# Feed-forward part of a two-layer sequence kernel: pairs of chunks on 64x64 tiles of the PE array

## The chip, the cores and the metric

The kernel runs on one core of one Trainium2 chip. The metric is the device time of one execution in microseconds (us); the time of a kernel is the median of its runs. PE is the matrix engine (TensorE), PEld its weight loads, DVE the vector engine, ACT the scalar engine, POOL GpSimd, SP the queue from which most loads are issued. All data are fp32.

## The reference

The input x is 4 batches x 512 time steps x 128 frequencies x 64 channels (a row of 8192 features for each time step). Layer 0 is a sequence block, layer 1 a spectral one. Cut to what matters:

```
# layer 0, for each batch
xn = layernorm(x);  k, v, r = xn@Wk, xn@Wv, sigmoid(xn@Wr)       # 8192 -> 64 each
states = scan(s = decay*s + k*v);  x = x + (r*states)@Wo          # projection, scan, attention
x = x + gelu(conv_freq(layernorm(x)))                             # 3 taps over frequency
x = x + layernorm(conv_time(layernorm(x)))                        # 3 causal taps over time, per feature
mid = gelu(x @ ffn_W1 + ffn_b1)                                   # 64 -> 256 for each (time, frequency)
x = x + (mid @ ffn_W2 + ffn_b2)                                   # 256 -> 64
# layer 1: moving average (25 steps) + 128 Fourier modes mixed over frequency, then back
```

The change is in the last two lines of layer 0.

## The kernel before

`layer0` keeps data with features on partitions. A chunk is 128 features (2 frequencies x 64 channels) x 512 time steps; there are 64 chunks a batch, and most steps take pairs of chunks (32 pairs). Layer 0 is cut into stages, each a Python generator that issues instructions and yields a weight: J `project` (8192 to k, v, r), Z `scan`, A `attend_and_convolve`, C `convolve_time`, O `open_feed` (residual of the first two pairs), F `feed_forward`. `in_turn` runs two of them side by side, always the one that is behind, with a small lead for the second stream. The order of matmuls is therefore written by hand; the instructions of the other engines are put in order by the scheduler, except those pinned with `keep_in_program_order`. The pairing of stages is:

| first stream | second stream |
|---|---|
| Z(0), A(0) | J(1), Z(1) |
| C(0) | A(1) |
| O(0), F(0) | J(2), Z(2) |
| C(1) | A(2) |
| O(1), F(1) | J(3), Z(3) |
| C(2) | A(3) |
| O(2), F(2) | C(3), O(3) |
| F(3) | nothing |

Then `layer1` runs, from DRAM.

**F before.** For each chunk c, `widen(c, m)` for m = 0, 1 multiplies each half of the chunk (one frequency, 64 channels, so 64 rows of the array) by 128 of the 256 middle features: two matmuls of 64 rows x 128 columns into the two banks of a double PSUM tile, m from pool `ps_m` (tile m) or `ps_c` (tile c), L718. ACT makes the GELU of 128x1024 into `mid` (L722, 4 buffers). `narrow(c-1)` multiplies back: four matmuls of 128 rows x 64 columns, summed over m, into the one bank of `ps_p` (tile pa, L729); DVE adds bias and residual into `x4t` (L734, `scalar_tensor_tensor`). `store(c-2)` transposes x4t in four 128x128 matmuls (tile pt, L743) into the bank s of `ps_s` if the attention stage does not hold it (`free_s`), else into that of `ps_p`; ACT copies them to `ob` (L752, or in halves L750), and POOL issues one DMA for each four chunks (L754). Between them `residual` (L686, L687 on DVE) and `add_residual` (L695 on ACT, L698 on DVE) make the input x3 two pairs ahead.

In F(0) and F(1) each second chunk also advances `convolve_ahead(b + 1)`: 14 pairs of the next time convolution, made early by DVE (L608, L611, L620) and ACT (L616), with the rows for it spread by PE into the bank of `ps_p` (L241). In C, `add_up` sums values and squares by matmuls with a block of ones (L251). In A, `convolve` uses tiles m and c too (L547 for the norm's correction, L556 for neighbouring halves with 64x64 weights, L561 for the chunk itself), and the sums go into bank s. The eight PSUM banks are: `ps_a` 2, `ps_c` 2, `ps_m` 2, `ps_s` 1, `ps_p` 1.

Of the kernel before, what the change touches and what calls it, by code (L numbers as in the profile page):

```python
# [16 lines left out]
P = 128  # L17
# [62 lines left out]
def layer0(ctx, tc, dram, x, xt, vecs, wkvr, wo, wdec, wconv, fbias, w1, fb1, w2, fb2, x4):  # L80
# [73 lines left out]
    tb_all = const.tile([P, NCH], F32, name="tb_all")  # L154
    fix = const.tile([P, NCH, 2], F32, name="fix")
# [12 lines left out]
    def prepare():  # L168
# [45 lines left out]
        t01 = rowp.tile([P, SL], F32, tag="rg", name="t01")[:, 0:P].rearrange("p (k c) -> p k c", k=2)  # L214
        t0, t1 = t01[:, 0, :], t01[:, 1, :]
        nc.vector.tensor_tensor(t0, vec[:, W0, :], vec[:, B3, :], ALU.mult)
        nc.vector.tensor_tensor(t1, vec[:, W1, :], vec[:, B3, :], ALU.mult)
        nc.vector.tensor_tensor(t1, t1, t0, ALU.add)
        nc.vector.tensor_scalar_mul(fix[:, :, 0], t1, -1.0)
        nc.vector.tensor_scalar_mul(fix[:, :, 1], t0, -1.0)  # L220
        nc.vector.tensor_tensor(tb_all, vec[:, W2, :], vec[:, B3, :], ALU.mult)
        nc.vector.tensor_tensor(tb_all, tb_all, t1, ALU.add)
        nc.vector.tensor_tensor(tb_all, tb_all, vec[:, TB, :], ALU.add)
        for k in (W0, W1, W2):
            nc.vector.tensor_tensor(vec[:, k, :], vec[:, k, :], vec[:, G3, :], ALU.mult)
# [91 lines left out]
    free_s = [True]  # L317
    held = [False]
# [193 lines left out]
    def attend_and_convolve(b):  # L512
# [62 lines left out]
        for i in range(NPR + 3):  # L575
# [8 lines left out]
            if 1 < i < NPR + 2:  # L584
                convolve(i - 2)
                yield 5.0
            if i == 3:
                st = ps_s.tile([P, SL], F32, tag="s", name="st")
                free_s[0] = False
# [39 lines left out]
    def convolve_ahead(b):  # L629


        rb, mb = yield from rows(of_p, *carried[b], "rm3")
        ahead[b] = rb, mb
        for i in range(AHEAD):
            xr = spare("x1", SL)
            normed(b, i, xr, xr, rb, mb, True)
            yield
            tapped(b, i, xr, spare("z", SL), True)
            yield
# [69 lines left out]
    def feed_forward(b):  # L709
        x3s = opened.pop(b)  # L710
        mids, x4s, obs = {}, {}, {}

        def widen(c, m):
            x3 = x3s[c // 2][:, c % 2, :]
            pm = c_bank() if m else two(ps_m, "m")
            for h in range(2):
                hs = slice(h * H, (h + 1) * H)
                nc.tensor.matmul(  # L718
                    pm[:, h, :], lhsT=w1_sb[hs, m * P : (m + 1) * P], rhs=x3[hs, :], start=True, stop=True
                )  # L720
            mid = mids[c, m] = bk.tile([P, 2, SL], F32, tag="mid", name="mid", bufs=4)
            nc.scalar.activation(mid, pm, AF.Gelu_apprx_tanh, bias=fb1_sb[:, m : m + 1])  # L722

        def narrow(c):
            pa = ps_p.tile([P, SL], F32, tag="p", name="pa")
            for m in range(2):
                mid = mids.pop((c, m))
                for h in range(2):
                    nc.tensor.matmul(  # L729
                        pa[h * H : (h + 1) * H, :], lhsT=w2_sb[:, m, :], rhs=mid[:, h, :],  # L730
                        start=(m == 0), stop=(m == 1),
                    )
            x4t = x4s[c] = bk.tile([P, SL], F32, tag="x4t", name="x4t", bufs=3)
            nc.vector.scalar_tensor_tensor(x4t, pa, fb2_sb, x3s[c // 2][:, c % 2, :], ALU.add, ALU.add)  # L734
            if c % 2:
                x3s.pop(c // 2)

        def store(c):
            x4t = x4s.pop(c)
            pool, tag = (ps_s, "s") if free_s[0] else (ps_p, "p")  # L740
            pt = pool.tile([P, NT, P], F32, tag=tag, name="pt")
            for t in range(NT):
                nc.tensor.transpose(pt[:, t, :], x4t[:, t * P : (t + 1) * P], ident)  # L743
            s = c // 4
            if c % 4 == 0:
                obs[s] = bk.tile([P, NT, SL], F32, tag="ob", name="ob")
            o = obs[s][:, :, c % 4 * P : (c % 4 + 1) * P]
            if c // 2 % 2:
                for h in range(2):
                    nc.scalar.copy(o[:, :, halves[1 - h]], pt[:, :, halves[h]])  # L750
            else:
                nc.scalar.copy(o, pt)  # L752
            if c % 4 == 3:
                nc.gpsimd.dma_start(  # L754
                    x4[b][:, s * SL : (s + 1) * SL].rearrange("(t p) d -> p t d", p=P), obs.pop(s)
                )

        early = None
        for c in range(NCH + 2):
            if c < NCH:  # L760
                widen(c, 0)
                widen(c, 1)
            i = c // 2 + 2
            if i < NPR:
                if c % 2:
                    x3s[i] = add_residual(b, i, *coming)
                else:
                    coming = residual(b, i)
            if 0 < c <= NCH:
                narrow(c - 1)  # L770
            if c > 1:
                store(c - 2)
            if b + 2 < B and c > 4 and c % 2:
                early = early or convolve_ahead(b + 1)
                next(early, None)
            yield 4.5
# [40 lines left out]
    def nothing(b):  # L817
# [7 lines left out]
        F: 4.5 * (NCH + 2), nothing: 1.0,  # L825
# [253 lines left out]
def _inputs(x, i):  # L1079
# [22 lines left out]
    for rows, parts in ((MODES, ("w_real", "w_imag")), (IMAG, ("w_imag", "w_real"))):  # L1102
# [14 lines left out]
        "fb1": i["ffn_b1"].reshape(2, P).T,  # L1117
        "w2": i["ffn_W2"].reshape(2, P, H).transpose(1, 0, 2),
# [22 lines left out]
```

## Time and profile before

| what | value |
|---|---|
| median of 3 runs | 3773.87 us (3772.81 to 3791.47) |
| span of the profiled execution | 3800.7 us; the page gives no other time of that execution |
| PE busy | 3636.3 us (96% of the span) |
| DVE, ACT, POOL busy | 2683.6, 1761.2, 513.3 us |
| F(0), F(1): first to last L718 matmul | 839.3 to 1224.2, 1498.0 to 1878.4 us |
| F(2) and F(3) | 2146.6 to 2788.0 us |
| layer 1 | from about 2796 us to the end |

An engine's busy time is the time in which at least one of its instructions runs. Matmuls are pipelined and their ends are modelled, so the record of a 512-wide matmul is longer (0.59 us) than the distance to the next on the same part of the array. An fp32 matmul of 512 columns leaves two records with one weight load each; a transpose leaves one. "64*128" after a matmul's tiles is the part of the array that it uses, rows*columns. Lines of the profile (L718) are lines of the kernel before.

### The profile page before, as it was taken

How to read it: one execution, taken by the hardware profiler on the slowest of the kernel's cores; microseconds unless marked ns; L12 is line 12 of the kernel's file. 1: busy time of each engine (PE TensorE's matmuls, PEld its weight loads, DVE VectorE, ACT ScalarE, POOL GpSimd, SP SyncE). 2: the span in 40 equal slices, each digit the busy share in tenths (PEclk: the TensorE clock that was granted, in tenths of full speed). 3: DMA queues.
4: the chain of work that ended last, by engine and by line, in shares of the span. 5: the costliest groups of instructions: out<-in, count | busy, mean ns of one | idle time of the engine just before them, and what ended most of it. 6: DMA issues, size and time to landing. Idle time of an engine off the chain costs nothing. (4 is left out here: it accounts for less than half of the span.)

```text
span 3800.7 us, 44873 instructions
## 1 busy us (share of the span) xinstructions
PE 3636.3 (96%) x15945; PEld 1345.5 (35%) x15945; DVE 2683.6 (71%) x3498; ACT 1761.2 (46%) x2491; POOL 513.3 (14%) x782
## 2 busy tenths in 40 slices
PE   9989999999999999999999988999989999999998
PEld 4433322223333223333322322333322843327533
DVE  4445559976777896677789799755567277892677
ACT  0013336645656565566656678867744210142100
POOL 0000012210011221011122221100012000131001
PEclk9999989999999899999999999999999999999999
DMA  9867647786874788787478677545567478993687
GB/s 310 272 203 242 229 146 264 254 288 241 287 280 169 247 285 287 251 278 278 172 258 282 205 249 262 202 155 177 183 222 246 146 236 295 309 294 140 205 296 264
DMA packets 429175, 912.80 MB, mean 240 GB/s; under 512 B 33240, under 2 KB 83608, under 8 KB 424856
## 3 DMA queue, kind: packets, MB, share of 16 engines
q1 hardware_dynamic: 351024, 636.87, 49.7%
q0 software_dynamic: 75776, 271.62, 20.5%
q8 instruction: 127, 2.08, 0.2%
q10 hardware_dynamic: 2152, 1.45, 0.1%
q14 instruction: 96, 0.79, 0.1%
HBM read 641.31 MB, written 268.50 MB: 239 GB/s over the span
## 5 line engine op out<-in xcount | busy, mean ns | idle before, releaser
L729 PE MATMUL pa<-mid,w_sb 128*64 128x512 f32 x2048 | 500.2, 609 | 37.2 <-DVE x4t L734 37.2
L734 DVE SCALAR_TENSOR_TENSOR x4t<-pa,fb_sb,x 128x512 f32<-128x512 f32 x252 | 188.4, 748 | 345.7 <-PE pa L729 345.6
L722 ACT ACTIVATE mid<-m,fb_sb 128x1024 f32<-128x1024 f32 x256 | 285.1, 1114 | 280.5 <-PE m L718 280.2
L718 PE MATMUL m<-x,w_sb 64*128 64x512 f32 x1008 | 290.4, 649 | 0.4 <-ACT mid L722 0.4
L722 ACT ACTIVATE mid<-c,fb_sb 128x1024 f32<-128x1024 f32 x256 | 283.2, 1106 | 1.5 <-PE c L718 1.5
L718 PE MATMUL c<-x,w_sb 64*128 64x512 f32 x1008 | 263.4, 596 | 1.3 <-ACT mid L722 1.3
L729 PEld LDWEIGHTS pa<-mid,w_sb 128*64 128x64 f32 x2048 | 125.0, 136 | 379.9 <-issue 250.8
L406 PE MATMUL a<-xp,wx 128*128 128x512 f32 x512 | 240.7, 596 | 0.5 <-DVE me L268 0.5
L986 ACT COPY two<-a 128x512 f32<-128x512 f32 x64 | 37.5, 586 | 425.0 <-PE a L981 425.0
L1009 PE MATMUL b<-xin,avg_sb 128*128 128x512 f32 x512 | 230.8, 593 | 2.3 <-DVE xin L1015 2.3
L1015 DVE TENSOR_TENSOR xin<-b,pm 128x512 f32<-128x512 f32 x256 | 159.1, 684 | 95.6 <-PE b L1012 80.7
L567 ACT ACTIVATE sq<-x 128x1024 f32<-128x1024 f32 x128 | 135.0, 1054 | 180.5 <-DVE x L564 180.5
L620 DVE SCALAR_TENSOR_TENSOR to<-kd,vec,to 128x510 f32<-128x510 f32 (+1 forms) x272 | 197.8, 746 | 16.0 <-ACT to L616 10.4
L695 ACT ACTIVATE kd<-kd,vec 128x512 f32<-128x512 f32 x256 | 193.3, 809 | 3.1 <-DVE kd L687 3.1
L891 DVE COPY xf<-b 128x256 f32<-128x256 f32 x128 | 54.4, 425 | 185.3 <-PE b L955 173.2
L912 DVE TENSOR_TENSOR uv<-xin 128x1024 f32<-128x1024 f32 x128 | 155.4, 1227 | 39.4 <-DMA xin<-x 18.9
L251 PE MATMUL st<-x,ones 128*32 128x512 f32 x512 | 169.4, 611 | 13.3 <-DVE x L564 13.1
L743 PEld LDWEIGHTS pt<-ident,x4t 128*128 128x128 f32 x1024 | 107.7, 141 | 208.7 <-ACT mid L722 152.5
L528 DVE TENSOR_TENSOR x<-a,xp 128x1024 f32<-128x1024 f32 x128 | 156.2, 1220 | 33.6 <-PE a L526 31.1
L620 DVE SCALAR_TENSOR_TENSOR z<-x,vec,z 128x511 f32<-128x511 f32 x240 | 175.8, 745 | 5.7 <-ACT z L616 2.3
L526 PE MATMUL a<-rst,wo_sb 64*128 64x512 f32 x512 | 153.1, 672 | 27.2 <-DVE x L528 23.2
L743 PE MATMUL pt<-ident,x4t 128*128 128x128 f32 x1024 | 168.8, 288 | 1.5 <-ACT ob L750 1.5
(241 smaller groups left out, 6532.8 us busy)
## 6 DMA issues: line engine op xcount, KB each, us to landing
xp<-in_xt SPq DMA_DIRECT2D x256, 512.0 KB
xin<-x SPq DMA_DIRECT2D x128, 1024.0 KB
kh<-to SPq DMA_DIRECT2D x156, 512.0 KB
x<-x POOLq DMA_DIRECT2D x128, 512.0 KB, 4.4
kx<-x SPq DMA_DIRECT2D x128, 512.0 KB
x<-ob POOLq DMA_DIRECT2D x64, 1024.0 KB, 6.3
out<-xin POOLq DMA_DIRECT2D x64, 1024.0 KB, 7.1
x<-x SPq DMA_DIRECT2D x96, 512.0 KB
```

The lines of the kernel that those rows point to most:

```text
L251: nc.tensor.matmul(st[32 * q : 32 * q + 32, :], lhsT=ones, rhs=src[:, j, :], start=first, stop=last,)
L406: nc.tensor.matmul(pa[:, k, :], lhsT=wq[:, j, k * P : (k + 1) * P], rhs=xp[:, j, :], start=first and j == 0, stop=last and j == 1,)
L528: nc.vector.tensor_tensor(x1, at, xp, ALU.add)
L620: tap = nc.vector.scalar_tensor_tensor(to[:, j, k:], xr[:, j, : SL - k], vec[:, w, c], to[:, j, k:], ALU.mult, ALU.add)
L695: tc.keep_in_program_order(nc.scalar.activation(d[:, j, :], d[:, j, :], AF.Identity, bias=vec[:, B4, c], scale=vec[:, G4, c]))
L718: nc.tensor.matmul(pm[:, h, :], lhsT=w1_sb[hs, m * P : (m + 1) * P], rhs=x3[hs, :], start=True, stop=True)
L722: nc.scalar.activation(mid, pm, AF.Gelu_apprx_tanh, bias=fb1_sb[:, m : m + 1])
L729: nc.tensor.matmul(pa[h * H : (h + 1) * H, :], lhsT=w2_sb[:, m, :], rhs=mid[:, h, :], start=(m == 0), stop=(m == 1),)
L734: nc.vector.scalar_tensor_tensor(x4t, pa, fb2_sb, x3s[c // 2][:, c % 2, :], ALU.add, ALU.add)
L743: nc.tensor.transpose(pt[:, t, :], x4t[:, t * P : (t + 1) * P], ident)
L1009: nc.tensor.matmul(po[j], lhsT=avg_sb[:, j, :], rhs=xin[:, j, :], start=True, stop=False)
L1015: nc.vector.tensor_tensor(by_n(xin[:, j, :]), by_n(po[j]), by_c(pm[j % 2][:, j // 2, :]), ALU.add)
```

## The change

F takes pairs of chunks and quarters of the middle features. `widen(i, q)` makes quarter q (64 features) for pair i: four matmuls of 64 rows x 64 columns, one for each row half h (frequency) and column half j (chunk of the pair), into bank h of tile m or c in turn (`unit`); the partitions of the tile are then 64 features of chunk 0 and 64 of chunk 1. `narrow(i, q)` takes the GELU back in four matmuls of 64 x 64: row half j, column half h, into one accumulator for each chunk (banks p and s), over four quarters. They alternate: widen 2, narrow 0, widen 3, narrow 1, widen 0 of the next pair, narrow 2, widen 1 of the next, narrow 3. The eight transposes of a pair come together at the head of an iteration into a tile m or c, one pair behind in F(0) and F(1), two behind in F(2) and F(3) (`lag`); ACT copies both chunks at once. F yields once for each pair. A flag `feeding` keeps the attention stage from bank s while F runs, and F waits until `free_s`. The rows of `convolve_ahead` go to a tile m or c. Weights w2 and bias fb1 are laid out by quarters, and two constant tables, `tb_all` and `fix`, now lie in rows of `vec` that are no longer needed.

```diff
-    tb_all = const.tile([P, NCH], F32, name="tb_all")
-    fix = const.tile([P, NCH, 2], F32, name="fix")
+    tb_all = vec[:, TB, :]
+    fix = vec[:, G3 : B3 + 1, :].rearrange("p k c -> p c k")
...
     free_s = [True]
+    feeding = [False]
...
+            while i == 3 and feeding[0]:
+                yield BLOCKED
             if i == 3:
                 st = ps_s.tile([P, SL], F32, tag="s", name="st")
...
-    def convolve_ahead(b):
-        rb, mb = yield from rows(of_p, *carried[b], "rm3")
+    def convolve_ahead(b, bank):
+        rb, mb = yield from rows(bank, *carried[b], "rm3")
...
     def feed_forward(b):
         x3s = opened.pop(b)
+        mids, x4s, obs, sums2 = {}, {}, {}, {}
+        lag = 1 if b + 2 < B else 2
+        turn = [0]
+        while not free_s[0]:
+            yield BLOCKED
+        feeding[0] = True
+
+        def unit():
+            turn[0] ^= 1
+            return two(ps_m, "m") if turn[0] else c_bank()
...
+        def widen(i, q):
+            x3 = x3s[i]
+            pm = unit()
             for h in range(2):
-                hs = slice(h * H, (h + 1) * H)
-                nc.tensor.matmul(
-                    pm[:, h, :], lhsT=w1_sb[hs, m * P : (m + 1) * P], rhs=x3[hs, :], start=True, stop=True
-                )
-            mid = mids[c, m] = bk.tile([P, 2, SL], F32, tag="mid", name="mid", bufs=4)
-            nc.scalar.activation(mid, pm, AF.Gelu_apprx_tanh, bias=fb1_sb[:, m : m + 1])
+                for j in range(2):
+                    nc.tensor.matmul(
+                        pm[halves[j], h, :], lhsT=w1_sb[halves[h], q * H : (q + 1) * H], rhs=x3[halves[h], j, :],
+                        start=True, stop=True,
+                    )
+            mid = mids[i, q] = bk.tile([P, 2, SL], F32, tag="mid", name="mid", bufs=4)
+            nc.scalar.activation(mid, pm, AF.Gelu_apprx_tanh, bias=fb1_sb[:, q : q + 1])
...
+        def narrow(i, q):
+            if q == 0:
+                sums2[i] = of_p(), ps_s.tile([P, SL], F32, tag="s", name="pb")
+            mid = mids.pop((i, q))
+            for h in range(2):
+                for j in range(2):
+                    nc.tensor.matmul(
+                        sums2[i][j][halves[h], :], lhsT=w2_sb[halves[j], q, :], rhs=mid[halves[j], h, :],
+                        start=q == 0, stop=q == 3,
+                    )
+            if q < 3:
+                return
+            x3 = x3s.pop(i)
+            if lag > 1:
+                pair = spare("wx", 4 * S + SL)[:, :, 0:SL]
+                x4s[i] = [pair[:, j, :] for j in range(2)]
+            else:
+                x4s[i] = [bk.tile([P, SL], F32, tag="x4t", name="x4t", bufs=3) for _ in range(2)]
+            for j, pa in enumerate(sums2.pop(i)):
+                nc.vector.scalar_tensor_tensor(x4s[i][j], pa, fb2_sb, x3[:, j, :], ALU.add, ALU.add)
+
+        def store(i):
+            pt = unit()
+            for j, x4t in enumerate(x4s.pop(i)):
+                for t in range(NT):
+                    nc.tensor.transpose(pt[:, j, t * P : (t + 1) * P], x4t[:, t * P : (t + 1) * P], ident)
...
+            if i % 2:
                 for h in range(2):
-                    nc.scalar.copy(o[:, :, halves[1 - h]], pt[:, :, halves[h]])
-            else:
-                nc.scalar.copy(o, pt)
-            if c % 4 == 3:
+                    nc.scalar.copy(o[:, :, :, halves[1 - h]], pt[:, :, :, halves[h]])
                 nc.gpsimd.dma_start(
                     x4[b][:, s * SL : (s + 1) * SL].rearrange("(t p) d -> p t d", p=P), obs.pop(s)
                 )
+            else:
+                nc.scalar.copy(o, pt)
...
+        widen(0, 0)
+        widen(0, 1)
+        for i in range(NPR + lag):
+            if i >= lag:
+                store(i - lag)
+            if i < NPR:
+                widen(i, 2)
+                narrow(i, 0)
+                widen(i, 3)
+                narrow(i, 1)
+                if i + 2 < NPR:
+                    coming = residual(b, i + 2)
+                if i + 1 < NPR:
+                    widen(i + 1, 0)
+                narrow(i, 2)
+                if i + 1 < NPR:
+                    widen(i + 1, 1)
+                if i + 2 < NPR:
+                    x3s[i + 2] = add_residual(b, i + 2, *coming)
+                narrow(i, 3)
+            if b + 2 < B and i > 1:
+                early = early or convolve_ahead(b + 1, lambda: unit()[:, 0, :])
                 next(early, None)
-            yield 4.5
+            yield 9.0 * (NPR + 1) / (NPR + lag)
+        feeding[0] = False
```

More of the change, by code (lines that the diff above doesn't have):

```diff
@@ L210, in prepare @@
                 nc.scalar.dma_start(cgr[q : q + 2, :, :], cg4[h, j])
-        t01 = rowp.tile([P, SL], F32, tag="rg", name="t01")[:, 0:P].rearrange("p (k c) -> p k c", k=2)
-        t0, t1 = t01[:, 0, :], t01[:, 1, :]
+        t012 = rowp.tile([P, SL], F32, tag="rg", name="t012")[:, 0 : 3 * NCH].rearrange("p (k c) -> p k c", k=3)
+        t0, t1, t2 = t012[:, 0, :], t012[:, 1, :], t012[:, 2, :]
         nc.vector.tensor_tensor(t0, vec[:, W0, :], vec[:, B3, :], ALU.mult)
@@ L218, in prepare @@
         nc.vector.tensor_tensor(t1, t1, t0, ALU.add)
+        nc.vector.tensor_tensor(t2, vec[:, W2, :], vec[:, B3, :], ALU.mult)
+        nc.vector.tensor_tensor(t2, t2, t1, ALU.add)
+        nc.vector.tensor_tensor(tb_all, vec[:, TB, :], t2, ALU.add)
+        for k in (W0, W1, W2):
+            nc.vector.tensor_tensor(vec[:, k, :], vec[:, k, :], vec[:, G3, :], ALU.mult)
         nc.vector.tensor_scalar_mul(fix[:, :, 0], t1, -1.0)
         nc.vector.tensor_scalar_mul(fix[:, :, 1], t0, -1.0)
[L221 to L225, printed above, removed]
     sums = {}
@@ L710, in feed_forward @@
         x3s = opened.pop(b)
[L711 to L715, printed above, removed]
-            for h in range(2):
-                hs = slice(h * H, (h + 1) * H)
-                nc.tensor.matmul(
-                    pm[:, h, :], lhsT=w1_sb[hs, m * P : (m + 1) * P], rhs=x3[hs, :], start=True, stop=True
-                )
-            mid = mids[c, m] = bk.tile([P, 2, SL], F32, tag="mid", name="mid", bufs=4)
-            nc.scalar.activation(mid, pm, AF.Gelu_apprx_tanh, bias=fb1_sb[:, m : m + 1])
@@ L724, in narrow @@
[L724 to L727, printed above, removed]
-                for h in range(2):
[L729 to L749, printed above, removed]
-                    nc.scalar.copy(o[:, :, halves[1 - h]], pt[:, :, halves[h]])
-            else:
-                nc.scalar.copy(o, pt)
-            if c % 4 == 3:
+        mids, x4s, obs, sums2 = {}, {}, {}, {}
@@ new lines, in store @@
+        def store(i):
[3 more added lines that the diff above has]
+                    nc.tensor.transpose(pt[:, j, t * P : (t + 1) * P], x4t[:, t * P : (t + 1) * P], ident)
+            s = i // 2
+            if i % 2 == 0:
+                obs[s] = bk.tile([P, NT, SL], F32, tag="ob", name="ob")
+            o = obs[s][:, :, i % 2 * 2 * P : (i % 2 + 1) * 2 * P].rearrange("p t (j w) -> p j t w", j=2)
+            pt = pt.rearrange("p j (t w) -> p j t w", t=NT)
+            if i % 2:
+                for h in range(2):
+                    nc.scalar.copy(o[:, :, :, halves[1 - h]], pt[:, :, :, halves[h]])
@@ L756, in store @@
                 )
+            else:
+                nc.scalar.copy(o, pt)
         early = None
[L759 to L763, printed above, removed]
-            if i < NPR:
[L765 to L774, printed above, removed]
+        widen(0, 0)
[3 more added lines that the diff above has]
+                store(i - lag)
+            if i < NPR:
+                widen(i, 2)
[14 more added lines that the diff above has]
+                early = early or convolve_ahead(b + 1, lambda: unit()[:, 0, :])
                 next(early, None)
-            yield 4.5
+            yield 9.0 * (NPR + 1) / (NPR + lag)
+        feeding[0] = False
     CHAIN = 6.0
@@ L824, in layer0 @@
         J: 2.0 * NPR, Z: 7 * CHAIN, A: 7.0 * NPR + 3 * CHAIN, C: 7.0 * (NPR + 2) + 3 * CHAIN, O: 4 * CHAIN,
-        F: 4.5 * (NCH + 2), nothing: 1.0,
+        F: 9.0 * (NPR + 1), nothing: 1.0,
     }
@@ L1116, in _inputs @@
         "w1": np.concatenate([i["ffn_W1"]] * 2, axis=0),
-        "fb1": i["ffn_b1"].reshape(2, P).T,
-        "w2": i["ffn_W2"].reshape(2, P, H).transpose(1, 0, 2),
+        "fb1": np.concatenate([i["ffn_b1"].reshape(4, H).T] * 2),
+        "w2": np.concatenate([i["ffn_W2"].reshape(4, H, H).transpose(1, 0, 2)] * 2),
         "fb2": np.concatenate([i["ffn_b2"]] * 2)[:, None],
```

## The prediction

> **What bounds the kernel now.** I read the page's busy times first, then busy time by stage, then PE's instructions in order of time, then who waited for whom. The page says that PE is the engine to look at:
>
> ```profile
> PE 3636.3 (96%) x15945; PEld 1345.5 (35%) x15945; DVE 2683.6 (71%) x3498; ACT 1761.2 (46%) x2491; POOL 513.3 (14%) x782
> ```
>
> A mean over stages with different limits is not enough, so I cut the span at the first and last matmuls of the feed-forward part (columns: stretch, its length, busy time of PE, PEld, DVE, ACT and POOL with instruction counts, clock, DMA share, GB/s):
>
> ```profile
> 839.00:1232.00 393.00, 387.62 (x1569) 146.38 (x1568) 284.59 (x386) 240.90 (x323) 38.77 (x47) 0.99 0.70 249
> ...
> 1498.00:1889.00 391.00, 387.33 (x1561) 145.91 (x1560) 281.61 (x380) 240.48 (x322) 38.99 (x47) 0.99 0.72 250
> ...
> 2146.00:2516.00 370.00, 330.06 (x1580) 114.38 (x1578) 322.31 (x360) 294.50 (x391) 64.06 (x82) 0.97 0.65 225
> 2516.00:2796.00 280.00, 278.19 (x1272) 101.18 (x1272) 150.93 (x150) 212.81 (x283) 11.33 (x16) 1.00 0.46 160
> ```
>
> These are F(0) (beside the projection of batch 2), F(1) (beside that of 3), F(2) (beside the time convolution of 3) and F(3) alone: 1434 us in all. In the first, second and fourth PE is busy 99%. In F(2) it is 89% and DVE 87%; there PE waited 34.7 us for one thing:
>
> ```profile
> PE pa L729 <- DVE x4t L734: 34.7, 29, 3.9
> ```
>
> PE busy is not PE useful. In F(3), one chunk runs from one m to the next (columns: start, length, engine, line, op, tiles, rows*columns of the array used, moving operand, records; a 512-wide fp32 matmul leaves two records):
>
> ```profile
> 2703.55 1.13 PE L718 MATMUL m<-x,w_sb 64*128 64x512 f32 x4
> 2704.51 1.02 PE L718 MATMUL c<-x,w_sb 64*128 64x512 f32 x4
> 2705.47 1.94 PE L729 MATMUL pa<-mid,w_sb 128*64 128x512 f32 x8
> 2707.34 0.65 PE L743 MATMUL pt<-ident,x4t 128*128 128x128 f32 x4
> 2707.92 1.13 PE L718 MATMUL m<-x,w_sb 64*128 64x512 f32 x4
> ```
>
> A chunk takes 4.37 us. One pass over 512 columns is 0.429 us (the chain of waits has L1009, 8 full-array records, at 3.43 us). The 16 widen and narrow records run two at a time, so 8 steps, 3.43 us; from m to pt it took 3.79. The rest is spent where the shape of the array changes: 64*128, 128*64, 128*128, three times a chunk. The trace also has 64*64 tiles (L556) and four abreast in long runs (L251):
>
> ```profile
> 1251.05 1.09 PE L556 MATMUL c<-z,wcs 64*64 64x512 f32 x8
> 1252.07 1.98 PE L561 MATMUL c<-z,wcs 128*128 128x512 f32 x4
> ...
> 1273.32 0.59 PE L251 MATMUL p<-to,ones 128*32 128x512 f32 x1
> ...
> 1273.75 0.59 PE L251 MATMUL p<-kh,ones 128*32 128x512 f32 x1
> ...
> 1274.17 0.59 PE L251 MATMUL p<-kh,ones 128*32 128x512 f32 x1
> ...
> 1274.60 0.59 PE L251 MATMUL st<-x,ones 128*32 128x512 f32 x1
> ```
>
> Eight 64*64 records between two other shapes took 1.02 us: two steps of four (0.86) and **0.16 for one change of shape**. L251 goes from sum to sum and from bank p to bank st at 0.43 a step: within a shape nothing is added.
>
> [...] The new code sends row half h of the widening to bank h and row half j of the narrowing to bank j; L556 is laid out so too and its four run together. [...] ACT is at 76% in F(3) already. [...] The new stream has 64 records in 6.86 us, 107 ns each; the trace has eight 64*64 records with short operands (L190) in 0.41 us, 51 ns each, so I charge nothing.
>
> **The change part by part.**
>
> *Shapes.* Per pair of chunks the array work stays: widening 16 matmuls (32 records, four abreast, 8 steps), narrowing the same, eight transposes. 16 x 0.429 = 6.86 us, as 2 x 3.43 before. Changes of shape fall from six a pair to two: into the transposes and out. (Beside the projection, its full-array matmuls now stand just ahead of the transposes and need no change between; beside the convolution of 3 the sums cost one more, before and after.) Four changes at 0.16 = **0.65 us a pair**. Cross-check for F(3): 6.86 + 0.16 + 0.58 (pt to m) + four more transposes at (0.66 - 0.29)/3 = 0.12 each is 8.08, against 8.74. 128 pairs: **-83 us** gross, 21 a stage.
>
> *Twice as many matmul and weight-load records:* hidden, since L251 loads four weights within each 0.43 us step. If that cover were gone it is the last rival.
>
> *ACT.* Four GELUs a pair stay (1.11 each), r (L695) stays (2 x 0.81). The two (or, with halves swapped, four) copies of a pair's transposes become one 128x1024 (between 0.58, the 128x512 row, and 1.16, two of them; I take 1.00 by L562, 128x1024 from PSUM) or two 128x512 (1.16). That is 7.1 to 7.2 us of a pair's 8.1 in F(3). In the new order the copy stands behind r; the third widening of the pair needs its bank, 2.8 us after the transposes began, and r and copy end at about 2.75. I charge 0.1 x 32 = +3 us.
>
> *F(0), F(1).* ACT also makes the taps of the convolution ahead (14 pairs in each stage). In the new order the first tap stands in front of the GELU of the pair's first widening, and waits for DVE, whose order there is x4t twice (1.5), x3, L608, L686, L611 (1.22 each): ready 6.6 us after the last narrowing. Tap (0.8) and GELU (1.0) end at 8.4; PE wants the bank back at 7.9 (projection 3.43, transposes 1.0, four units of 0.86). 0.6 x 28 = +17 us (0 if DVE runs ahead, 40 if its loads are late).
>
> *Lag of one pair in F(0), F(1):* the transposes follow the narrowing whose x4t they read. The projection (3.43 us) covers DVE's 1.6 us in 28 pairs a stage. In the last five it is gone, and only scan matmuls (about 1 us) stand there: 0.6 x 10 = +6 us, 0 to 20.
>
> *F(2).* DVE needs five 128x1024 operations (1.22) and six 128x512 (0.75) a pair: 10.6 us, PE only 8.1 + 1.0 for the sums. A pair took 370/32 = 11.6. So DVE is next. Two waits on x4t a pair become one, with 2.9 us (sums, transposes, one widening) against 1.6 of x4t. I take 11.1 a pair, 15 us of the 21: +6; bounds 10.6 (gain 31) and 11.6 (none).
>
> *The two accumulators* take bank p and bank s, so the attention stage's sums must wait until a feed-forward ends; in the order of matmuls that come out, no attention step of the next batch lay inside one, before or after: zero. If one did it would wait, not run, and other steps take its place. *Constants:* tb_all and fix move into vec; the same number of 128x64 DVE operations (about 0.2 us), hidden behind the first projection. *Queues:* the same loads on SP (x2 and the causal output, one each a pair) and 64 stores on POOL; the loads of two projection steps come together and have three buffers; zero, and at most a few us.
>
> Sum: -83 + 3 + 17 + 6 + 6 = **-51 us**. The profiled execution spans 3800.7 us, 0.7% over the median of 3773.87; the page names no other time of it. A saving in us moves from one to the other: 3800.7 - 51 = 3750 there, 3723 at the median, -1.4%.
>
> **Rivals.**
>
> *All of it lands* (ACT's taps early, F(2) at DVE's 10.6): -83 - 10 = 3681 at best, about 3690 likely. For: PE busy 99% in three of four stages. Against: ACT at 88% in F(3).
>
> *ACT and DVE eat it.* GELUs late by 1.5 us in the tap pairs (+42), F(2) at 11.6 (+21), F(3)'s copy late by 0.2 (+6): -83 + 69 = 3760, no change. For: PE's wait on x4t in F(2), and DVE's 10.6 of 11.6. Against: in F(0) PE waited for DVE 5.3 us in all. That the change did nothing is the same time: the order of matmuls does change, but work that another engine sets would not show it.
>
> *Slower:* the 0.16 us belongs to every new group of four tiles and not to the shape. Place: each of the eight widen or narrow units of a pair. 8 x (0.86 + 0.16) + 1.06 = 9.2 us against 8.74, +0.46 x 128 = +59, less some 15 that F(2)'s DVE hides: 3818. For: m and c take 0.96 each here, not 0.86, though both are 64*128. Against: L251 at 0.43 across banks and sums; m pays entering, c leaving. It decides from 0.08 us a unit.
>
> **How the numbers follow.** Forecast 0.68, all lands 0.10, eaten 0.14, slower 0.08. Predicted time 3723. Range 3688 to 3768: it takes in "all lands" and "eaten", and leaves out the slower case and the ends of the bounds. 0.5% is 19 us, about what a measurement of this kernel can tell from no change. Faster by more: the first two and a small part of "eaten", 0.79; within: 0.13; slower: 0.08.
>
> **What would show it.** In F(3), a pair at 8.0 to 8.3 us from transposes to transposes, with steps of 0.43 through widenings and narrowings; F(3) 258 to 266 us. F(0) and F(1) at 375 to 387, with PE waits on ACT in the widening where taps run. F(2) at 340 to 365, DVE over 90%. Wrong would be a unit over 0.94 us, or PE busy under 95% in F(0), F(1) or F(3).

## The result, and the profile after

The changed kernel takes 3755.1 us in the median of 4 runs (3751.9 to 3761.8), the kernel before 3773.34 us in the runs beside it: ratio 0.9945, 95% interval 0.9927 to 0.9964. It is faster by about 18 us where 51 were forecast. The profiled execution spans 3752.0 us and took 3753.95. Compared once more (`after_again` below) it gives 0.9928, interval 0.9902 to 0.9954, about 23 us.

PE's busy time fell by 64 us (3636.3 before). The spans of the two profiled executions differ by more than the medians do, 3800.7 against 3752.0 us, in part because the profiled execution of the kernel before reached F(0) late: at 839.3 us, where `e2_coarse` and `e10_cut_before`, the same kernel up to there, took 824.4 and 822.5. So the spans are not compared. The busy times after:

```profile
PE 3572.1 (95%) x20041; PEld 1376.3 (37%) x20041; DVE 2676.7 (71%) x3498; ACT 1762.1 (47%) x2299; POOL 512.5 (14%) x782
```

Cut by stage (columns as before: stretch, length, busy time of PE, PEld, DVE, ACT and POOL, clock, DMA share, GB/s), with F(0), F(1), F(2), F(3) in this order:

```profile
820.00:1217.00 397.00, 377.47 (x2586) 154.91 (x2584) 285.47 (x391) 245.07 (x277) 38.53 (x48) 0.97 0.73 247
1479.00:1867.00 388.00, 371.02 (x2578) 149.94 (x2576) 280.06 (x378) 242.51 (x274) 36.24 (x45) 0.98 0.74 252
2129.00:2490.00 361.00, 324.26 (x2598) 129.68 (x2600) 320.05 (x360) 289.69 (x340) 65.69 (x81) 0.95 0.68 231
2490.00:2753.00 263.00, 262.88 (x2304) 103.03 (x2296) 150.46 (x150) 211.54 (x236) 12.07 (x16) 0.99 0.49 171
```

F(3) fell from 280 to 263 us. F(2) fell by 9. F(0) and F(1), where a third of the saving was expected, stand at 397 and 388 against 393 and 391, and PE is busy 95 and 96% there instead of 99%. Two numbers serve as yardsticks from here on, because they leave out the start of the kernel and layer 1. The first is the stretch from the first widening of F(0) to that of F(2), two feed-forwards and the convolutions after them: 1307.3 us before (1310.2 in `e10_cut_before`, which differs only from F(2) on), 1308.7 after (1302.7 in `after_again`, 1303.4 in `e10_cut_after`). One kernel's stretch thus differs by up to 6 us from execution to execution, and each number is of one execution. The second is F(2) with F(3), to the last transposes: 648.5 before, 623.5 after. **By these the second gained 25 us and the first between nothing and 8**, together somewhat more than the medians' 18 to 23, as one execution may.

F(3) shows the new stream undisturbed. PE's instructions in order of time, one pair from transposes (L762) to transposes; L730 widens, L743 narrows:

```profile
2605.61 1.09 PE L762 MATMUL m<-ident,wx 128*128 128x128 f32 x8
2606.63 1.09 PE L730 MATMUL c<-x,w_sb 64*64 64x512 f32 x8
2607.54 0.60 PE L743 MATMUL p<-mid,w_sb 64*64 64x512 f32 x2
2607.55 0.60 PE L743 MATMUL pb<-mid,w_sb 64*64 64x512 f32 x2
2607.97 0.60 PE L743 MATMUL p<-mid,w_sb 64*64 64x512 f32 x2
2607.98 0.60 PE L743 MATMUL pb<-mid,w_sb 64*64 64x512 f32 x2
2608.42 1.09 PE L730 MATMUL m<-x,w_sb 64*64 64x512 f32 x8
...
2613.73 1.09 PE L762 MATMUL c<-ident,wx 128*128 128x128 f32 x8
```

A pair takes 8.12 and 8.18 us in turn, against 8.74. The narrowing takes 0.88 us from its first record to the next widening, two steps of 0.43 to 0.45: next to nothing is added between groups of four.

F(0) shows where it went. PE's waits from 820 to 1217 us (columns: what PE was about to do, whom it waited for, us in total, times, longest):

```profile
PE a L476 <- DVE wx L472: 4.1, 1, 4.1
PE c L730 <- ACT mid L735: 3.7, 12, 0.6
PE a L241 <- POOL rs L233: 3.5, 1, 3.5
PE m L730 <- ACT mid L735: 2.7, 3, 1.2
PE a L502 <- DVE hs L496: 2.5, 1, 2.5
PE a L503 <- DVE hs L497: 1.4, 1, 1.4
```

Four of the six are steps of the scan Z(2), the stage that follows the projection as second stream. In F(1) the scan Z(3) holds PE up by 7.1, 3.4 and 1.9 us; the longest two, with a line left out between them:

```profile
PE a L494 <- DVE rst L489: 7.1, 1, 7.1
...
PE a L468 <- DVE wx L472: 3.4, 1, 3.4
```

The scan's waits come to about 12 us in each of the two stages. In the kernel before, one scan step waited in each, for 2.9 us in F(0) and 2.4 in F(1). The tail of F(0) in order of time, each wait in brackets at the end of the line that it held up:

```profile
1153.05 2.08 PE L241 MATMUL a<-ident,rs 128*128 128x128 f32 x8 [3.54 <-POOL rs L233]
1155.80 2.08 PE L241 MATMUL a<-ident,mean 128*128 128x128 f32 x8 [0.68 <-ACT rm L285]
1157.67 1.92 PE L762 MATMUL c<-ident,x4t 128*128 128x128 f32 x8
1159.52 1.99 PE L730 MATMUL m<-x,w_sb 64*64 64x512 f32 x8
...
1178.25 1.12 PE L468 MATMUL a<-kvrg,sel 128*128 128x512 f32 x2
1183.43 2.07 PE L476 MATMUL a<-kvrg,sel 64*128 64x512 f32 x2 [4.06 <-DVE wx L472]
1185.43 1.97 PE L762 MATMUL c<-ident,x4t 128*128 128x128 f32 x8
```

Two scan steps stand back to back between two whole pairs of the feed-forward. L476 follows an L468 directly and waits for what DVE makes from it (L472). The first L241 waits for what POOL makes at the scan's start, and the second for ACT's copy of the first. In the kernel before, the second L241 and the first L467 (its L468) came 5.3 us apart (1177.92 and 1183.18) with a chunk between them. The second thing to see is the length of the lines that follow a wait: transposes of 1.92 and 1.97 us and a widening of 1.99, nearly twice the 1.04 and 1.09 that they take in the pairs with projection (the transposes 1.22 right behind the L468 at 1167.66 us). **Here waits of 3.5 and 4.1 us are followed by matmuls at about half speed**, so they cost about twice: after the first two waits, 4.2 us together, the four lines shown take 8.07 us where 4.3 to 4.6 is usual (an L241 without a wait before it takes 1.06 to 1.16), and the granted clock is 0.51 from 1153 to 1162 us and 0.50 from 1183 to 1189. It shows as well after the waits of 2.5 and 1.4 us that L502 and L503 have one after the other: the transposes behind them take 1.97 us, at a clock of 0.50. Two waits of 1.2 us before widenings in the same tail are not followed by it (1.09 us each).

From one set of transposes to the next, the last five pairs of F(0) and F(1) took 57.8 and 57.3 us before, 74.9 and 66.8 after (70.6 and 66.5 in `after_again`), with the same projection and scan matmuls between them: 22 to 27 us lost in ten pairs.

### The profile page after: what moved, and what is told of

Its sections match the earlier page's. It is cut to its first block, busy times and chain, and to the rows that moved or that the text cites. A ratio compares the mean times of both kernels' runs of the same rounds, so it can differ in the third digit from the quotient of the medians.

```text
span 3752.0 us, 52992 instructions
## 1 busy us (share of the span) xinstructions
PE 3572.1 (95%) x20041; PEld 1376.3 (37%) x20041; DVE 2676.7 (71%) x3498; ACT 1762.1 (47%) x2299; POOL 512.5 (14%) x782
## 5 line engine op out<-in xcount | busy, mean ns | idle before, releaser
L743 PE MATMUL p<-mid,w_sb 64*64 64x512 f32 x2048 | 559.1, 596 | 15.5 <-DVE wx L756 14.3
L743 PE MATMUL pb<-mid,w_sb 64*64 64x512 f32 x2048 | 531.6, 596 | 0.7 <-DVE wx L756 0.7
L730 PE MATMUL c<-x,w_sb 64*64 64x512 f32 x2016 | 280.8, 610 | 16.1 <-ACT mid L735 11.9
L730 PE MATMUL m<-x,w_sb 64*64 64x512 f32 x2016 | 280.7, 609 | 6.7 <-ACT mid L735 4.5
L743 PEld LDWEIGHTS p<-mid,w_sb 64*64 64x64 f32 x2048 | 158.7, 135 | 287.8 <-issue 248.9
L623 DVE SCALAR_TENSOR_TENSOR to<-kd,vec,to 128x510 f32<-128x510 f32 (+1 forms) x272 | 197.1, 742 | 12.5 <-ACT to L619 11.2
L251 PE MATMUL st<-x,ones 128*32 128x512 f32 x512 | 168.9, 605 | 11.5 <-DVE x L565 11.5
L701 DVE TENSOR_TENSOR x<-kd,kx 128x1024 f32<-128x1024 f32 x126 | 154.0, 1222 | 32.5 <-ACT kd L698 32.5
L756 DVE SCALAR_TENSOR_TENSOR x4t<-p,fb_sb,x 128x512 f32<-128x512 f32 x64 | 47.9, 748 | 177.2 <-PE pb L743 177.1
```

What stands on the lines that cost most here:

```text
L251: nc.tensor.matmul(st[32 * q : 32 * q + 32, :], lhsT=ones, rhs=src[:, j, :], start=first, stop=last,)
L623: tap = nc.vector.scalar_tensor_tensor(to[:, j, k:], xr[:, j, : SL - k], vec[:, w, c], to[:, j, k:], ALU.mult, ALU.add)
L701: nc.vector.tensor_tensor(x3, d, x2, ALU.add)
L730: nc.tensor.matmul(pm[halves[j], h, :], lhsT=w1_sb[halves[h], q * H : (q + 1) * H], rhs=x3[halves[h], j, :], start=True, stop=True,)
L743: nc.tensor.matmul(sums2[i][j][halves[h], :], lhsT=w2_sb[halves[j], q, :], rhs=mid[halves[j], h, :], start=q == 0, stop=q == 3,)
```

## The experiments

The first theory: **turns**. F now yields once a pair (weight 9.0) instead of once a chunk (4.5). When the projection is used up, five pairs before the end of F(0) and F(1), the scan's chain of small steps alternates with blocks twice as long, and two of its steps fall into one gap. Rivals: the **lag** of one pair for the transposes, which the forecast named; ACT's **taps**; the **shape** changes being worth less than 0.16 us. In kernels that add lines above, line numbers stand one to three higher.

**e1_half.** Half turns once the projection of batch b+2 has ended (`over` is filled at the end of `project`):

```diff
+        weight = 9.0 * (NPR + 1) / (NPR + lag)
         for i in range(NPR + lag):
+            part = 1.0
...
                 narrow(i, 1)
+                if b + 2 in over:
+                    part = 0.5
+                    yield part * weight
...
-            yield 9.0 * (NPR + 1) / (NPR + lag)
+            yield part * weight
```

> Theory (scan tail): once the projection is used up, the coarse turns of a whole pair put the scan's dependent steps beside too little other work; PE waits (19 us in F(0), 17 in F(1)) and then runs at half clock. With turns of half a pair there, F(0) and F(1) get 10 to 18 us shorter each, the sum of PE's waits on DVE and POOL there falls below 8 us each, and the median is 3723 to 3737. Rival (taps in front of GELUs on ACT): those stalls sit in the pairs with projection, so this edit moves nothing, 3750 to 3760. Rival (lag of one pair): nothing moves either, since the transposes still follow their narrowing.

Measured: 3748.18 us, ratio 0.9919, interval 0.9891 to 0.9947, which overlaps that of the changed kernel; the whole missed its 3723 to 3737. F(1) fell from 386.8 to 374.2 us (first widening to last transposes). F(0) did not move: 395.6 against 396.1. Of the scan's long waits there only that on L241 was left (3.5 us), and another took their place, on x4t:

```profile
1195.85 1.09 PE L764 MATMUL c<-ident,x4t 128*128 128x128 f32 x4 [5.93 <-DVE x4t L758]
...
1223.99 1.97 PE L764 MATMUL c<-ident,x4t 128*128 128x128 f32 x8 [3.86 <-DVE x4t L758]
```

The waits on x4t come to 11.3 us in F(0), where the changed kernel had none. So turns explain F(1), and in F(0) another wait stood hidden behind them: that of the transposes for x4t. Whether the lag makes it, or DVE being held up by something else, is for the next runs.

**e2_coarse.** The kernel before, with its own tiles, but turns of two chunks in F(0) and F(1):

```diff
-            yield 4.5
+            if b + 2 >= B:
+                yield 4.5
+            elif c % 2:
+                yield 9.0
```

> The kernel before, on its old tiles, with turns of two chunks in F(0) and F(1) only. Theory (scan tail): the coarse turns alone cost 10 to 18 us in each of the two, so 3793 to 3808 against 3773 before, with PE waits on the scan's DVE and POOL steps at the end of F(0) and F(1). Rivals (taps, lag, or the new tiles themselves cost the gain): no change, 3768 to 3778.

Measured: 3814.94 us, ratio 1.0084, interval 1.0053 to 1.0116. F(0) rose from 392.5 to 403.0, F(1) from 390.5 to 400.3, F(2) with F(3) stayed at 648.1. PE's waits are those of the changed kernel one line up, in F(0):

```profile
PE a L475 <- DVE wx L471: 4.5, 1, 4.5
PE a L241 <- POOL rs L233: 2.0, 1, 2.0
PE a L502 <- DVE hs L496: 1.6, 1, 1.6
```

and in F(1):

```profile
PE a L493 <- DVE rst L488: 5.8, 1, 5.8
PE a L467 <- DVE wx L471: 2.5, 1, 2.5
```

Turns of that length cost about 10 us a stage with nothing else changed, on the old tiles. The median lies above the 3793 to 3808 expected, and the profiled execution (3801.06) is the quickest of the four, so the stages of the others may have lost more.

**e3_split.** Two changes of shape put back in: four transposes, a widening, then the other four.

```diff
         for i in range(NPR + lag):
             if i >= lag:
-                store(i - lag)
+                turned(i - lag, 0)
             if i < NPR:
                 widen(i, 2)
+            if i >= lag:
+                turned(i - lag, 1)
+                store(i - lag)
+            if i < NPR:
                 narrow(i, 0)
```

`turned(i, j)` makes the four transposes of chunk j, `store` the copies.

> The changed kernel with a pair's eight transposes in two groups of four, the second after the pair's first widening: two more changes of shape a pair, 0.16 us each. If a change of shape costs 0.16 us and lies on the path, +0.33 x 32 = +10 us in F(0), F(1) and F(3) each and up to as much in F(2): 3785 to 3797. If the gain of the change was not the shapes, 3750 to 3762.

Measured: 3876.76 us, ratio 1.0258, interval 1.023 to 1.0285: +122 us on the changed kernel, a miss by a factor of three. The price of the shape shows locally in F(3):

```profile
2704.84 0.66 PE L765 MATMUL c<-ident,wx 128*128 128x128 f32 x4
2705.43 1.09 PE L730 MATMUL m<-x,w_sb 64*64 64x512 f32 x8
2706.45 0.66 PE L765 MATMUL c<-ident,wx 128*128 128x128 f32 x4
2707.03 0.64 PE L743 MATMUL p<-mid,w_sb 64*64 64x512 f32 x1
```

From the first transposes to the narrowing it takes 2.19 us; in the changed kernel eight transposes and a widening took 1.93 (2605.61 to 2607.54 above). Two more changes cost 0.26, 0.13 each against the 0.16 of the forecast. Most of the rest is a wait that the edit made. The transposes' tile is held over a widening more, and PE waits for the copies of it, in F(2) and F(3) for:

```profile
PE c L730 <- ACT ob L777: 35.1, 29, 2.4
PE m L730 <- ACT ob L782: 29.7, 29, 2.0
```

These waits come to 65 us in the 64 pairs of F(2) and F(3), where the shapes at 0.26 a pair come to 17, and to 39 us in F(0) and F(1). The local price stands; the total of this kernel says nothing on it.

**e4_taps.** The convolution ahead is issued in the middle of a pair, so that its taps stand behind the GELUs that PE waits for:

```diff
                 if i + 1 < NPR:
                     widen(i + 1, 1)
+                ahead_step(i)
...
-            if b + 2 < B and i > 1:
-                early = early or convolve_ahead(b + 1, lambda: unit()[:, 0, :])
-                next(early, None)
+            if i >= NPR:
+                ahead_step(i)
```

> The changed kernel with the step of the convolution ahead called in the middle of the pair, so that in ACT's order the taps stand behind two GELUs of the pair instead of in front of the first. If the tap stalls (0.25 to 0.6 us in each of 28 pairs) are the loss, F(0) and F(1) get 5 to 8 us shorter each, 3740 to 3746. If the scan tail is the loss, at most 3750 to 3757, and the pair with taps still takes about 11.6 to 12.0 us.

Measured: 3835.12 us, ratio 1.0131, interval 1.0098 to 1.0164; F(0) 428.5, F(1) 423.3. A miss with the wrong sign. DVE now makes its taps ahead of x4t, and with a lag of one pair PE waits for that in pairs that were free of it:

```profile
PE c L762 <- DVE x4t L756: 21.8, 11, 2.0
```

One such wait, and the half speed behind it:

```profile
930.53 1.27 PE L762 MATMUL c<-ident,x4t 128*128 128x128 f32 x8 [1.95 <-DVE x4t L756]
931.73 1.98 PE L730 MATMUL m<-x,w_sb 64*64 64x512 f32 x8
```

This run makes a wait of its own and so can't weigh the taps. The changed kernel can: its pairs with taps take 12.0 to 12.1 us, those without 11.5, which is close to what the forecast charged, so the taps are not what it missed. The lag of one pair holds in F(0) and F(1) only while DVE does x4t first.

**after_again.** The changed kernel as it is, beside the next three.

> The changed kernel as it is, as the yardstick for the runs beside it: 3751 to 3762 us again. F(0) 392 to 398, F(1) 384 to 390, F(2) and F(3) together 620 to 626; the last five pairs of F(0) 70 to 78 us, of F(1) 63 to 70.

Measured: 3758.0 us, ratio 0.9928, interval 0.9902 to 0.9954; F(0) 391.8, F(1) 385.8, F(2) with F(3) 622.7.

**e5_pin.** e1_half, with one DVE wait for a load moved out of the tail of F(0):

```diff
-            scale_weights(0, ws[0])
+            scale_weights(0, ws[0], True)
```

> Half turns as in e1_half, and the scaling of the first weights of the next projection is kept in program order, so that DVE does not meet its load in the tail of F(0). If that load is what made the transposes wait for x4t in e1_half (10.4 us there), F(0) falls by 8 to 13 us against e1_half's 395.6, F(1) stays at 374 and the whole is about 3738. If the lag of one pair is too short in the tail whatever DVE does, F(0) stays within 3 us of 395.6 and the x4t waits stay at about 10 us.

Measured: 3752.8 us, ratio 0.9924, interval 0.9901 to 0.9948. F(0) fell to 386.8 as expected of the load, F(1) is 375.4. The whole did not follow, and missed its 3738: in the stretch from F(0) to F(2) it stands at 1295.5 us, as e1_half does at 1295.9, and where the 9 us of F(0) were lost again stays open. The waits on x4t in F(0) fell from 11.3 to 7.3 us, and 4.4 of these stand before the last transposes. So the load made a part of the wait and not the rest.

**e6_halff2.** e1_half with half turns in F(2) as well (`if b + 2 in over or b == 2`).

> Half turns as in e1_half, and in F(2) too, where the second stream is the time convolution of batch 3. If turns of a whole pair are what cost F(2) the 6 us that the forecast missed there (every fifth pair takes 13 to 15 us against 9.8 to 10.9), F(2) falls from 361 to 353 to 357. If DVE's work sets F(2), it stays at 359 to 363; if half turns bring the sums and the transposes closer to what they wait for, it rises by up to 8.

Measured: 3766.91 us, ratio 0.9969, interval 0.9957 to 0.9982. F(2) with F(3) rose from e1_half's 619.7 to 650.2, far beyond the 8 us expected at most. In F(2) the narrowing waits for the accumulators, which x4t reads:

```profile
PE p L745 <- DVE wx L758: 39.8, 15, 5.2
```

Turns of a whole pair are no loss in F(2); there they cover DVE's x4t. In these kernels longer turns cost time where the other stream is the scan's chain of small steps, and not where it is the time convolution.

**e9_share.** Whole turns, but the projection is issued faster and the scan over more pairs: `(J, 0.80), (Z, 0.20)` instead of 0.88 and 0.12 beside F(0) and F(1).

> The changed kernel with whole turns; only the projection is issued faster beside F(0) and F(1) (0.80 instead of 0.88 of the stage), so that the scan's small steps spread over eight or nine pairs instead of five, one to a turn. If two of those steps back to back in one turn are the loss, the waits on L241, L468, L476, L494 and L502 fall under 4 us a stage, F(0) and F(1) fall by 10 to 17 and 6 to 10 us, and the whole is 3730 to 3740. If the bare tail itself is the loss (pairs without projection, with the transposes one pair behind), more such pairs cost more: x4t waits appear, and the stages stay or rise by up to 8 us.

Measured: 3751.34 us, ratio 0.9911, interval 0.9885 to 0.9936. F(1) fell to 375.6, the scan's waits were gone from both stages. F(0) stayed at 392.6, with 10.4 us of wait on x4t (5.2 of it at one place, 4.4 before the last transposes) and 4.3 on the scaled weights. It gives the same picture as e1_half, by another way of separating the scan's steps.

**e11_share_pin.** e9_share with the line of e5_pin.

> Whole turns with the projection issued faster (e9_share), and the scaling of the next projection's first weights kept in program order as in e5_pin. If the two waits of e9_share in F(0), 5.2 us on x4t and 4.3 us on the scaled weights, come from DVE meeting a load, both go: F(0) falls by 7 to 10 us against 392.6 and F(1) stays at 375.6; the whole is 3735 to 3748. If the wait on x4t is the lag of one pair in the bare tail, F(0) falls by no more than 5 us.

Measured: 3751.79 us, ratio 0.9919, interval 0.9903 to 0.9935; F(0) 390.5, F(1) 375.6. F(0) fell by 2, as expected of the lag, but not cleanly. The wait of 5.2 us on x4t did go, so that one was the load's; the one on the scaled weights stayed at 4.3, and a wait on ACT's mid grew to 3.5 us. The last transposes of F(0) again wait 4.4 us for x4t.

**e7_lag2.** e1_half, and in the tail the transposes follow two pairs behind, as in F(2) and F(3):

```diff
-            if lag > 1:
+            if lag > 1 or b + 2 in over:
                 pair = spare("wx", 4 * S + SL)[:, :, 0:SL]
...
-            if i >= lag:
-                store(i - lag)
+            late = b + 2 in over or lag > 1
+            if done < NPR and done <= i - 1 - late:
+                store(done)
+                done += 1
```

> Half turns as in e1_half, and once the projection is over the transposes follow two pairs behind, with x4t in the buffers that the projection's weights leave free; the next projection's first weights are thereby loaded and scaled after the stage. If what is left in the tail after e5_pin is the lag (2.8 us of waits on x4t in F(0), 0.9 in F(1)), F(0) falls by 2 to 4 us against e5_pin's 386.8 (first widening to last transposes) and F(1) by about 1 against 375.4, with no wait on x4t. If the lag is of no matter once DVE is free, both stay within 1 us, and the last pair may take up to 8 us more for transposes that nothing covers.

Measured: 3724.5 us, ratio 0.9847, interval 0.9827 to 0.9867. F(0) 387.5, F(1) 380.4: those spans did not fall as expected. Scan and attention steps now stand between the last transposes. The stretch from F(0) to F(2) did, to 1284.4 us. The buffers `wx` that hold x4t here are also those into which the next projection's weights are loaded, so that this load comes later, by a time that was not shown; the next kernels separate the two.

**e12_lag2_whole, e14_lag2_xp, e7_again.** The lag of two with whole turns; with half turns; both with x4t in the projection's input buffers (`spare("xp", SL)`), which leaves the weights' loads alone; and e7_lag2 again.

> Whole turns as in the changed kernel; only the transposes follow two pairs behind once the projection is over, with x4t in the buffers of the projection's input. If the turns are the loss and the lag comes second, the scan's waits (L241, L468, L476, L494, L502, L503: about 12 us a stage) stay, F(0) and F(1) stay within 4 us of 392 and 386, and the whole is 3748 to 3760. If the lag is the loss, the whole is 3728 to 3740.

> Half turns and the lag of two in the tail as in e7_lag2, but with x4t in the buffers of the projection's input, so that the next projection's first weights are loaded as early as in the changed kernel. If half turns and lag made e7_lag2's 3724.5, this one gives 3722 to 3732 too. If the later load of those weights was the cause, it gives 3740 to 3752.

> e7_lag2 once more, beside the others: 3718 to 3734 again if its 3724.5 was no accident of four runs; F(0) 385 to 390, F(1) 378 to 382, the two stretches from the first widening of F(0) to that of F(2) 1280 to 1290 us.

| ratio to before (interval), stretch F(0) to F(2) | transposes one pair behind | two pairs behind in the tail |
|---|---|---|
| turn of a pair | changed kernel 0.9945 (0.9927 to 0.9964), 0.9928 (0.9902 to 0.9954); 1308.7, 1302.7 us | e12 0.9922 (0.9907 to 0.9937); 1304.3 us |
| half turns in the tail | e1 0.9919 (0.9891 to 0.9947), e5 0.9924 (0.9901 to 0.9948); 1295.9, 1295.5 us | e14 0.9876 (0.9864 to 0.9889), e7_again 0.9878 (0.9865 to 0.9891); 1280.6, 1283.9 us |

Medians: e12 3758.45, e14 3735.46, e7_again 3736.14 us, beside each other. e7_lag2's own 0.9847 is more than its later run gives, and 3736.14 misses the 3718 to 3734 expected of it, so I take the table's. e12's profiled execution took 3768.36 us, the slowest of its five, so its median says more than its stretch. The lag alone brings nothing that shows, half turns alone 7 to 13 us in the stretch and too little to tell in the whole. Both together bring 22 to 23 us in the median on the lag alone, and 12 to 15 in the stretch on half turns alone. e14 lies between the two ranges named for it, but no slower than e7_again beside it, so the later load is no part of it. PE's waits in F(0) of e12, the lag of two alone, show why it doesn't help: x4t isn't among them, as it wasn't in the changed kernel, and the scan's are still there (the first line, ACT's mid before widenings, is left out).

```profile
...
PE a L478 <- DVE wx L474: 5.6, 1, 5.6
PE a L241 <- POOL rs L233: 3.5, 1, 3.5
PE a L504 <- DVE hs L498: 2.5, 1, 2.5
PE a L505 <- DVE hs L499: 1.6, 1, 1.6
```

The stretch in two halves, for the changed kernel and then for e14_lag2_xp (the column behind the five engines is PE's clock):

```profile
820.50:1479.60 659.10, 632.98 (x3944) 228.18 (x3943) 496.73 (x611) 391.19 (x478) 90.28 (x120) 0.96 0.75 256
1479.60:2129.20 649.60, 613.48 (x3909) 220.53 (x3908) 493.40 (x598) 389.97 (x472) 89.13 (x120) 0.96 0.73 250
```

```profile
823.50:1472.30 648.80, 625.02 (x3945) 222.75 (x3944) 496.90 (x611) 391.36 (x478) 89.50 (x120) 0.98 0.77 260
1472.30:2104.10 631.80, 605.02 (x3911) 217.94 (x3910) 493.37 (x598) 389.61 (x472) 88.82 (x120) 0.98 0.76 257
```

The clock rises from 0.96 to 0.98 and PE is idle for 51 us (stretch less busy time) instead of 62: fewer waits, and less half speed behind them. Not all are gone: in F(0) of e14 L241 still waits 3.5 us for POOL, and the narrowing once 4.3 us for the accumulator that x4t reads.

**e13_all.** e7_lag2 with the faster projection of e9_share.

> e7_lag2 with the projection issued faster as well (0.80 for 0.88). If the scan's steps still stand too close in e7_lag2 (9.4 us of waits on L241, L496 and L529 in F(0)), spreading them gives another 3 to 8 us: 3716 to 3722. If half turns already spread them enough, the bare tail only grows longer and it is 3724 to 3735.

Measured: 3753.99 us, ratio 0.9918, interval 0.99 to 0.9937. That is 18 us slower than e7_again beside it, and a miss on both expectations. Its profiled execution can't say where: it took 3738.91 us, the quickest of six and as long as that of e7_again (3738.42), with 11 us more in the stretch (1294.6) and as many less elsewhere. So spreading the scan still further brought nothing, and why it costs stays open.

**e10_cut_before, e10_cut_after.** One DVE operation a pair left out in F(2) alone, in each of the two kernels, to see whether DVE sets F(2):

```diff
-        nc.vector.tensor_tensor(d, d, pair_of(mb), ALU.subtract)
+        if b != 2:
+            nc.vector.tensor_tensor(d, d, pair_of(mb), ALU.subtract)
```

> The kernel before with the same subtraction left out in F(2) alone. If DVE sets F(2), it falls from 370 to 338 to 352, less far than the changed kernel, because PE with its six changes of shape a pair is next. If DVE sets nothing, it stays over 360.

> The changed kernel without one DVE operation (the subtraction of the mean, 128x1024, 1.22 us, once a pair) in F(2) alone; this part of the computation is left out there. If DVE sets F(2), so that the new shape cannot show there, F(2) falls from 361 to 320 to 335, and the new shape's lead over e10_cut_before grows from 9 us to 15 to 22. If turns or the start of the stage set F(2), it stays over 345 and the lead stays at 9.

Measured: medians 3785.3 us (ratio 0.9995) for the kernel before, 3751.78 (0.9919, two runs) for the changed one. From the first widening of F(2) to that of F(3) the kernel before went from 367.1 to 369.1 us, the changed one from 360.4 to 348.8. The lead of the new tiles grew from 6.7 to 20.3 us, within the 15 to 22 expected, but by luck: neither kernel fell as far as expected, and the one before not at all. DVE's busy time in F(2) fell there by 30 us (321.7 to 291.2) without shortening it, so DVE's load alone doesn't set it. PE's waits on x4t stay (34.7 us without the cut); what sets them instead is not shown:

```profile
PE pa L730 <- DVE x4t L735: 30.2, 23, 3.3
```

In the changed kernel the same waits, 14.3 us without the cut, fall by half:

```profile
PE p L744 <- DVE wx L757: 7.5, 6, 1.3
```

## Why the prediction was right in direction and wrong in size

*Shapes, 0.65 us a pair: right.* F(3) runs at 8.12 and 8.18 us a pair in turn against the 8.08 worked out and 8.74 before; F(3) at 263 us lies in its 258 to 266. In F(0) and F(1) pairs without taps take 11.53 us against 12.18. A single change of shape came out at 0.13 us in e3_split, not 0.16.

*Twice the records, and the slower rival: no cost.* A unit takes 0.86 to 0.91 us, below the 0.94 that would have refuted the forecast.

*ACT's copy in F(3), +3: the sum fits, the wait isn't seen.* With the shapes it made -17.8; -17 was measured (280 to 263). But PE's waits from 2490 to 2753 us have no line at all, so that the copy cost anything is not shown.

*Taps, 0.6 us in 28 pairs: right in size.* Pairs with taps take 12.0 to 12.1 us, 0.5 more than those without; in the kernel before both took 12.18. PE waits on ACT's mid in the widening, as foreseen, but only 0.3 us a time (3.7 us in 12 waits on c L730 in F(0)). The forecast's own figures give 8.4 - 7.9 = 0.5, and its DVE steps (1.5 and four of 1.22) add up to 6.4, not 6.6.

*Lag of one pair, "only scan matmuls (about 1 us) stand there: 0.6 x 10 = +6 us, 0 to 20": this is the step that failed.* With the 0.65 a pair, the last five pairs of F(0) and F(1) should have come out even (-6.5 + 6). They lost 22 to 27 us. The term asked what PE does while x4t is made, and took the scan's steps as cover; it did not ask what the scan's steps themselves wait for when they come in twos. That F yields half as often was in the diff and was given no cost. The runs show that the place was right and the mechanism wrong: in the changed kernel PE doesn't wait for x4t there at all, but about 12 us a stage for the scan's inputs from DVE and POOL, and runs at half speed after the long waits (granted clock 0.50 and 0.51 behind those of 4.1 and 3.5 us in F(0)). The charge was about five times too small (28 to 33 us in place of 6). Turns of a pair stand in front (e2_coarse: 10 us a stage on the old tiles), and the wait that the term meant shows only behind them, once the turns are halved (e1_half: 11.3 us on x4t in F(0), a part of it DVE held up by a load). With both mended (e14_lag2_xp) the stretch F(0) to F(2) gains 27 us on the kernel before, where the forecast with its taps and its 6 us came to 19, and the changed kernel itself gained 8 at most.

*F(2), 11.1 us a pair and a gain of 15: half right.* It runs at 360/32 = 11.3 and gained 7 to 9 us, the first from widening to widening, the second by the stretches of the table. DVE was taken to set the pace at 10.6 a pair. It doesn't set it alone: the quickest pairs with one step of the convolution take 9.7 us before and 9.8 after, and the second pair after each double step takes 12 to 16, which the cut in e10_cut_after brings to 11.2. A light pair of the changed kernel (columns as in the table by stage) has DVE nearly full at 9.67 us:

```profile
2243.38:2253.15 9.77, 9.28 (x85) 3.16 (x84) 9.67 (x12) 8.90 (x11) 1.43 (x2) 1.00 0.89 317
```

With the cut such a pair still takes 9.8 us, with DVE at 8.96. PE's 9.28 us and its waits of up to 0.6 on tiles that ACT has not copied yet make up the pair. "DVE over 90%" was wrong too: 320.05 of 361 us is 89%.

*Accumulators in banks p and s, constants, queues: zero.* None shows among PE's longest waits, apart from those for x4t to free the accumulators in F(2) (14.3 us). No run tests these terms by themselves.

In sum, of the 28 to 33 us that were forecast and did not come, the tails account for 22 to 27 and F(2) for 6 to 8. The rival "eaten by ACT and DVE" named 3760, near the 3755 measured, but through GELUs 1.5 us late in pairs with taps; those waits were 0.3 us on average. It was near for the wrong reason. The signs named beforehand showed the miss in part: F(0), forecast at 375 to 387 us, came out at 396, and F(1) at the end of the range with 387; PE was busy 95.1 and 95.6% there, just above the 95% below which the forecast was to be wrong.

## What to carry to other kernels

Where two streams are interleaved by hand, the length of a turn is a cost of its own: when a stage's unit doubles, look at every stretch where the partner is a chain of small dependent steps, and ask of each of its steps what it waits for and what stands between. One wait can hide another at the same place: mending turns or lag alone hardly showed in the whole, and both together came to 1.2% less than the kernel before. And longer turns are not bad as such: in F(2) the whole pair covers DVE, and half turns cost 30 us.

## What the runs showed of the hardware beyond that

In F(0) waits of PE of 3.5 and 4.1 us, and of 2.5 and 1.4 us in short succession, were followed by matmuls of nearly twice the length (transposes of 1.92 and 1.97 instead of 1.04 to 1.25 us, widenings of 1.96 to 1.99 instead of 1.09) at a granted clock of 0.50 to 0.51. Even one of 1.95 us in e4_taps was (the widening behind the transposes took 1.98), while one of 1.9 us in F(1), at 1810 us, was not (the transposes took 1.04, the widening 1.09), nor were those of 1.2 us in the tail of F(0). A list of waits alone thus showed only about half of what the first two cost (4.2 us of wait, 3.4 to 3.8 of half speed). Four 64*64 tiles over 512 columns kept steps of 0.43 to 0.45 us through widenings and narrowings that alternate between two pairs of banks.
